# Selective scan: a different order of work ahead of the first scan, and other slots for the layer norm of later rows

## The chip, the cores and the metric

The kernel runs on one core of a Trainium2 chip. The metric is the device time of one execution in microseconds (us), as the median of several runs. A core has five engines with queues of their own, each of which works strictly in the order of its queue: PE (TensorE, matrix products), DVE (VectorE), ACT (ScalarE, activation functions), POOL (GpSimd) and SP (SyncE, which here only issues transfers). They wait for one another through semaphores.

## The reference

The program is a chain of four layers on a tensor of 2 images x 128 channels x 64 x 64 pixels: an attention layer, a convolution layer with deformed sampling, three residual steps of 3x3 convolutions, and a selective scan. The change lies in the last one. Cut to what matters, for an image x of L = 4096 pixels and C = 128 channels, run in four pixel orders:

```
xn = (x - mean(x)) * rsqrt(mean((x - mean(x))**2) + 1e-5) * w + b   # over the 128 channels
xh, z = split(xn @ W_in.T)                   # 256 channels each
xh = silu(causal_conv4(xh))                  # along the order
dt, B, C = split(xh @ W_xp.T)                # 8, 16 and 16 columns
dt = softplus(dt @ W_dt.T + b_dt)            # 256 channels
h[t] = exp(dt[t] * A) * h[t-1] + dt[t] * B[t] * xh[t]     # 256 channels x 16 states
y[t] = sum over states (h[t] * C[t]) + xh[t] * Dp
out  = (y * silu(z)) @ W_out.T
```

The four results are fused by one more product and added to x.

## The kernel before, in words

`layer3` (from line 1121) holds the scan. An image is cut into NBLK = 8 *blocks* of 512 pixels (8 image rows); with 2 images and 4 orders there are 64 blocks, worked off in one row: blocks 0 to 31 are image 0, 32 to 63 are image 1. Of an image, two orders go along the rows and two along the columns. The normalized image lies in two tiles: `xn`, by rows, and `xt`, by columns. Image 0 is normalized into `xn` and turned into `xt` by copies (`turn`, L1260); image 1 the other way round.

**Layer norm of one block of rows** is a chain of eight parts over four engines: `ln_mean` (PE, L1216, a product with a matrix of 1/128), `ln_less` (DVE, L1226, x minus mean), `ln_square` (ACT, L1229), `ln_var` (PE, L1233), `ln_log` (ACT, L1237), `ln_root` (ACT, L1240), `ln_scale` (POOL, L1243, the product of x minus mean and the root), `ln_store` (ACT, L1252). `ln_mean` and `ln_var` write to the PSUM tile called `da`, which rotates through three buffers and is also the one that the scan's decay factors use.

**The front of a block** makes what its scans need: `conv` (PE, L1294), `conv_silu` (ACT, L1299, with a table load before and one after), `xproj` (PE, L1318), `xproj_copy` (ACT, L1324 and L1326), `bc_store` (transfer of B and C to DRAM, L1330), `delta` (PE, L1345), `softplus` (ACT, four activations, L1351 to L1354), `sum_parts` (PE, L1359), `sum_copy` (ACT, L1362), `spread` (POOL, L1367, dt times xh), `xproj_rest` and `rest_copy` (PE L1336 and L1337, ACT L1340), `zproj` and `zproj_silu` (L1306, L1312). `spread_store` writes dt and dt times xh of one half of 128 channels to DRAM (L1372, 512 KB), and `spread_load` reads them back in eight transfers (L1381, 256 KB each), so that each partition holds one channel and one state of a group of four. `copies` reads B or C back, each row onto 32 partitions, in four transfers a group (L1401).

**The scan.** Each block has 8 *groups* (2 halves of channels x 4 groups of states), each of four scans. A group takes: `weights` (PE, L1391, B onto the partitions through PSUM), `db_dve` and `db_pool` (DVE L1412 and POOL L1421 share the product of B and dt times xh: the table `ND` says how many of four quarters are DVE's, for the eight groups 4, 0, 1, 4, 4, 4, 0, 4), `expo` (ACT, L1429, four decay factors), `scan` (DVE, L1438, four), `keep` (ACT, L1443, the last states, to `hl`), `cmul` (POOL, L1448, the states times C, over all four quarters), `sums` (PE, L1456). `gate`, `project` and `finish` end a block.

**The order is written out by hand**: inside `tc.manual_schedule()` each engine gets its instructions in program order. The main loop runs over all 512 groups and a few steps more; step k is group k % 8 ("slot") of block i = k // 8. In its slots the front of block i+1 is worked on (`front_pe`, `front_act`, `front_pool`, `transfers`), and from slot 5 on the convolution of block i+2. `expo` runs two scans ahead (AHEAD = 2); in its rotation of three `da` buffers a layer norm takes one whenever `ln_mean` or `ln_var` is due. `next_norm` says which rows' layer norm, if any, goes beside block i: in the kernel before these are the eight of image 1, beside blocks 22 to 29.

Ahead of the loop stands the *prologue*: a loop over t = 0 to 9 takes all eight layer norms of image 0, one behind the other, with the front of block 0 laid between them (slot = t - 2), and then the convolution of block 1. Five of the six sets of `copies` of block 0, `db_pool(1)` and the first two `expo` follow. The second half's `spread_load` of block 0 is issued in slot 0 of the main loop.

Of the kernel before, what the change touches and what calls it, by code (L numbers as in the profile page):

```python
# [25 lines left out]
NBLK = L // BLK  # L26
# [1094 lines left out]
def layer3(g, I, out):  # L1121
# [12 lines left out]
    with ExitStack() as ctx:  # L1134
# [70 lines left out]
        xn = a.tile([P, HW + 2 * HB, HW], F32, name="xn")  # L1205
        xt = a.tile([P, L + 2 * HC], F32, name="xt")
        N = {}


        def ln_tile():  # L1210
# [5 lines left out]
            nc.tensor.matmul(N[k, "mean"], onesm, interior(g, b, k * RB, RB), start=True, stop=True)  # L1216

        def ln_less(b, k):
            if b == 0:

                t = wk.tile([P, 4, BLK], F32, name="db")
                N[k, "xc"], N[k, "sq"] = t[:, 0, :], t[:, 1, :]
            else:
                N[k, "xc"] = ck.tile([P, BLK], F32, name="xc", bufs=1)
                N[k, "sq"] = ck.tile([P, BLK], F32, name="sq", bufs=1)
            nc.vector.tensor_sub(img(N[k, "xc"]), interior(g, b, k * RB, RB), img(N[k, "mean"]))  # L1226

# [100 lines left out]
        def bc_store(i):  # L1328
            S[i]["bx"] = dr.tile([2 * N_STATE, BLK], F32, name="bx")
            nc.sync.dma_start(S[i]["bx"], S[i]["xd"][: 2 * N_STATE])  # L1330
# [38 lines left out]
        def spread_store(i, hf):  # L1369

            S[i]["dx", hf] = dr.tile([P, 2, BLK], F32, name="dx")
            nc.sync.dma_start(S[i]["dx", hf], S[i].pop(("dd", hf)))  # L1372
# [11 lines left out]
        def weights(k):  # L1384

            i, hf, ng = groups[k]
            G[k] = {}
            if ND[hf][ng] == 0:
                return
            pb = psb.tile([P, BLK], F32, name="pbc")  # L1390
            nc.tensor.matmul(pb, sel[:, ng].rearrange("p j c -> p (j c)"), S[i]["bc"], start=True, stop=True)  # L1391
            G[k]["pb"] = pb
# [15 lines left out]
        def db_dve(k):  # L1408
            i, hf, ng = groups[k]
            n = ND[hf][ng]  # L1410
            if n:
                nc.vector.tensor_tensor(  # L1412
                    db_tile(k)[:, :n, :], G[k].pop("pb").unsqueeze(1).to_broadcast([P, n, BLK]),
                    S[i]["d4", hf][:, 1, :n, :], ALU.mult,
                )

        def db_pool(k):
            i, hf, ng = groups[k]
            n = ND[hf][ng]
# [113 lines left out]
        def front_pe(i, slot):  # L1533
            if i < NBK:
                if slot == 0:
                    xproj(i)
                elif slot == 1:
                    delta(i, 0)
                    delta(i, 1)
                elif slot == 2:  # L1540
                    sum_parts(i, 0)
                elif slot == 3:
                    sum_parts(i, 1)
                    xproj_rest(i)
                elif slot == 4:
                    zproj(i)
            if i + 1 < NBK:
                if slot == 5:
                    begin(i + 1)
                elif slot == 6:  # L1550
                    conv(i + 1, 1)

        def front_pool(i, slot):
            if i < NBK:
                if slot in (3, 4):
                    spread(i, slot - 3)

        def next_norm(i):

            b, k = divmod(i, 4 * NBLK)  # L1560
            k -= 4 * NBLK - 2 - NBLK
            return (b + 1, k) if b + 1 < NB and 0 <= k < NBLK else None

        with tc.manual_schedule():
            tc.keep_in_program_order(nc.scalar.preload_act_table_set("natural_log_exp_and_others"))
            nc.scalar.activation(am, am, AF.Exp)
            nc.vector.tensor_scalar(am, am, -1.0, None, ALU.mult)
            nc.vector.memset(xt[:, :HC], 0.0)
            nc.vector.memset(xt[:, HC + L :], 0.0)
            nc.vector.memset(xn[:, HB - 1, HW - HC :], 0.0)  # L1570
            nc.vector.memset(xn[:, HB + HW, :HC], 0.0)

            for t in range(NBLK + 2):
                slot = t - 2
                if slot == 6:
                    for k in range(2):
                        weights(k)
                    db_dve(0)
                    db_pool(0)
                if slot >= 0:  # L1580
                    front_pe(0, slot)
                    front_act(0, slot)
                    front_pool(0, slot)
                if slot == 1:
                    bc_store(0)
                elif slot in (3, 4):
                    spread_store(0, slot - 3)
                    if slot == 3:
                        spread_load(0, 0)
                        copies(0, "b", 0)  # L1590
                        copies(0, "c", 0)
                if t < NBLK:
                    for part in (ln_mean, ln_less, ln_square):
                        part(0, t)
                if 0 <= t - 1 < NBLK:
                    for part in (ln_var, ln_log, ln_root, ln_scale, ln_store):
                        part(0, t - 1)
                if t == 1:
                    begin(0)
                    conv(0, 1)  # L1600
                    conv_silu(0)
            for ng in range(1, NNG):
                copies(0, "b", ng)
                copies(0, "c", ng)
            db_pool(1)
            units = [(k, q) for k in range(len(groups)) for q in range(4)]
            AHEAD = 2
            for u in range(AHEAD):
                expo(*units[u])
            for k in range(len(groups) + 7):  # L1610
                i, slot = divmod(k, 8)
                live = k < len(groups)
                more = k + 1 < len(groups)
                ended = 1 <= k <= len(groups)
                transfers(i + 1, slot)
                if k + 2 < len(groups):
                    weights(k + 2)
                norm = next_norm(i)
                for q in range(4):
                    if slot == 6 and q == 3 and 1 <= i <= NBK:  # L1620
                        finish(i - 1)
                    if norm and slot == 3 and q == 3:
                        ln_log(*norm)
                    if 4 * k + q + AHEAD < len(units):
                        expo(*units[4 * k + q + AHEAD])
                    if norm and q == 0:
                        if slot == 0:
                            ln_mean(*norm)
                        elif slot == 3:
                            ln_var(*norm)  # L1630
                    if q == 0 and ended:
                        keep(k - 1)
                    if live:
                        scan(k, q)

                    for j, hf in (((k - 6) // 8, 0), ((k - 10) // 8, 1)):
                        if q == 1 and 8 * j + 6 + 4 * hf == k and 0 <= j < NBK:
                            gate(j, hf)
                if norm and slot == 0:
                    ln_less(*norm)  # L1640
                if more:
                    db_dve(k + 1)
                if ended:
                    cmul(k - 1)
                if k + 2 < len(groups):
                    db_pool(k + 2)

                if slot == 5 and 0 <= k - 2 < len(groups):
                    sums(k - 2)
                if slot == 5 and 1 <= i <= NBK:  # L1650
                    project(i - 1)
                front_pe(i + 1, slot)
                front_act(i + 1, slot)
                front_pool(i + 1, slot)
                if norm:
                    if slot == 1:
                        ln_square(*norm)
                    elif slot == 3:
                        ln_root(*norm)
                    elif slot == 4:  # L1660
                        ln_scale(*norm)
                    elif slot == 6:
                        ln_store(*norm)
                if live:

                    if slot == 6 and i % (4 * NBLK) < NBLK // 2:
                        for n in range(2):
                            turn(blocks[i][0], 2 * (i % (4 * NBLK)) + n)

                if slot != 5 and 0 <= k - 2 < len(groups):  # L1670
                    sums(k - 2)
# [160 lines left out]
```

## Time and profile before

| | |
|---|---|
| median of 3 runs | 5844.72 us (5840.14 to 5851.18) |
| the profiled execution, its own time | 5845.92 us |
| its span, first to last instruction | 5844.1 us |
| end of the layer before (last activation into `xa`) | 2453.66 us |
| first scan (L1438) | 2523.73 us |
| block 0's last gate (L1465) | 2585.33 us |
| a usual block, gate to gate | 51.56 us |
| nine blocks from 3612.62 to 4097.33, among them those with a layer norm | 484.71 us |

Times inside the execution are counted from the start of its span. The gate of a block's second half is read at slot 2 of the next block, so "block by block" below means from one such gate to the next. In the lists of waits, "A <- B: x, n, y" says that A waited for B for x us in n waits, the longest y us. In a timeline each line has start, duration, engine, line, operation and names, with the idle time of the engine before it and what ended it in brackets.

### The profile page before, as it was taken

To read this page: it belongs to the slowest core of one execution; us is meant where nothing else is said; L and a number is where in the kernel's file an instruction comes from. 1 tells how busy PE (TensorE), PEld (TensorE's weight loads), DVE (VectorE), ACT (ScalarE), POOL (GpSimd) and SP (SyncE) were. 2 spreads that over 40 slices of the span, in tenths; PEclk is the share of its full clock that TensorE was granted. 3 is DMA by queue.
4 is the path that set the end of the run, shared out by engine and by line. 5 is a ranking of instruction groups with operands and counts; after the bars stand their busy time and mean duration, and the time that the engine had idled before them with its cause. 6 is when DMAs were issued, how large, how long until landed. Compare 5 with 4: busy or idle time off the path is not lost.

```text
span 5844.1 us, 57551 instructions
## 1 busy us (share of the span) xinstructions
PE 4898.7 (84%) x19110; PEld 1732.8 (30%) x19110; DVE 4430.6 (76%) x4138; ACT 3829.3 (66%) x5499; POOL 3621.2 (62%) x1136
## 2 busy tenths in 40 slices
PE   7999999989978779877777878777787777778776
PEld 3333333334434334322222222222222222222221
DVE  5333333355124589679999999999999999999998
ACT  4888888840025521277777777777777777777775
POOL 5111111100010021079999999999999999999998
PEclk8999999999989889988888888888888888888886
DMA  5000001030056300055555565555555565555564
GB/s 156 19 19 19 19 19 33 1 59 1 1 101 112 76 12 0 6 136 130 136 130 131 142 141 130 121 133 143 137 135 128 131 141 141 133 131 132 134 141 101
DMA packets 333105, 541.88 MB, mean 93 GB/s; under 512 B 66384, under 2 KB 121184, under 8 KB 331712
## 3 DMA queue, kind: packets, MB, share of 16 engines
q1 hardware_dynamic: 329664, 534.58, 39.3%
q10 hardware_dynamic: 3136, 3.56, 0.2%
q8 instruction: 151, 2.47, 0.2%
q14 instruction: 154, 1.26, 0.1%
HBM read 448.81 MB, written 89.13 MB: 92 GB/s over the span
## 4 chain that ended last, share of the span: by engine, by line
DVE 50%; PE 37%; issue 5%; POOL 3%; DMA 2%; ACT 2%; SPq 1%; DVEq 0%; POOLq 0%; ACTq 0%
DVE db L1438 36%; DVE db L1412 12%; PE ps L287 11%; PE acc L303 9%; PE m L1052 6%; PE m L566 5%; PE acd L812 2%; DVE gt L1465 1%; PE m L526 1%; POOL db L1448 1%; PE pf L775 1%; POOL db L1421 1%; PE pc L663 1%; DMA hats<-pos 1%; SPq L748 1%
## 5 line engine op out<-in xcount | busy, mean ns | idle before, releaser
L1448 POOL TENSOR_TENSOR db<-db,c 128x2048 f32<-128x2048 f32 x512 | 2309.6, 4530 | 57.1 <-ACT hl L1443 52.0
L1438 DVE TENSOR_TENSOR_SCAN db<-da,hl,db 128x512 f32<-128x512 f32 x1792 | 2155.0, 1263 | 47.6 <-ACT da L1429 9.5
L1429 ACT ACTIVATE da<-dd,am 128x512 f32<-128x512 f32 x2048 | 1402.1, 688 | 824.3 <-DVE db L1438 814.5
L293 ACT ACTIVATE e<-ps 128x1024 f16<-128x1024 f32 x1024 | 992.3, 1021 | 135.7 <-PE ps L287 123.9
L1456 PE MATMUL py<-db,fold 128*32 128x512 f32 x4096 | 618.1, 689 | 234.8 <-POOL db L1448 231.9
L1421 POOL TENSOR_TENSOR db<-b,dd 128x2048 f32<-128x2048 f32 (+1 forms) x192 | 799.1, 4162 | 0.0
L1412 DVE TENSOR_TENSOR db<-pbc,dd 128x2048 f32<-128x2048 f32 (+1 forms) x384 | 767.3, 1998 | 0.6 <-PE pbc L1391 0.6
L314 DVE RECIPROCAL rec<-acc 32x512 f32<-32x512 f32 x64 | 214.9, 3358 | 640.3 <-PE acc L303 640.3
L321 POOL TENSOR_TENSOR parts<-parts 32x512 f32<-32x512 f32 x64 | 80.4, 1256 | 976.3 <-DVE parts L320 976.3
L287 PE MATMUL ps<-q,k 32*128 32x512 f32 x4096 | 656.4, 643 | 3.5 <-DVE flag L250 2.7
L303 PE MATMUL acc<-e,v 128*128 128x512 f16 x2048 | 532.2, 383 | 0.0
L1052 PE MATMUL m<-v,u 128*128 128x512 f32 x864 | 378.6, 601 | 50.6 <-DVE v L1021 50.6
L1359 PE MATMUL pm<-dd,ident 128*128 128x512 f32 x512 | 362.0, 845 | 4.6 <-ACT dd L1352 4.4
L1391 PE MATMUL pbc<-bc,sel 64*128 64x512 f32 x384 | 209.8, 546 | 162.8 <-DVE db L1412 162.6
L1318 PE MATMUL pm<-u,wxp 128*72 128x512 f32 x256 | 197.6, 917 | 175.0 <-ACT u L1299 175.0
L303 PEld LDWEIGHTS <-v 128*128 128x128 bf16 x2048 | 158.6, 97 | 510.6 <-issue 389.4
L1438 DVE TENSOR_TENSOR_SCAN db<-da,db 128x512 f32<-128x512 f32 x256 | 292.5, 1204 | 18.7 <-ACT da L1429 12.1
L287 PEld LDWEIGHTS ps<-q,k 32*128 32x128 f32 x4096 | 229.6, 183 | 228.3 <-issue 170.0
L1456 PEld LDWEIGHTS py<-db,fold 128*32 128x32 f32 x4096 | 90.4, 114 | 623.8 <-POOL db L1448 364.9
L566 PE MATMUL m<-comb,w 64*128 64x512 f32 (+4 forms) x1296 | 269.9, 575 | 0.0
L1294 PE MATMUL pm<-xn,wcs 128*128 128x512 f32 x512 | 236.9, 606 | 22.3 <-ACT xa L1483 7.5
L686 POOL TENSOR_SCALAR yt<-y 32x512 f32<-32x512 f32 x8 | 18.2, 2271 | 381.7 <-DVE y L677 381.3
(317 smaller groups left out, 6026.7 us busy)
## 6 DMA issues: line engine op xcount, KB each, us to landing
dd<-dx SPq DMA_DIRECT2D x1024, 256.0 KB, 6.4
dx<-dd SPq DMA_DIRECT2D x128, 512.0 KB, 3.4
c<-bx SPq DMA_DIRECT2D x1024, 64.0 KB, 2.1
hats<-pos SPq DMA_DIRECT2D x136, 256.0 KB, 9.7
b<-bx SPq DMA_DIRECT2D x512, 64.0 KB, 4.5
q<-qd SPq DMA_DIRECT2D x32, 512.0 KB, 7.4
w<-in_conv0T SPq DMA_DIRECT2D x18, 288.0 KB, 8.5
q<-in_x SPq DMA_DIRECT2D x8, 512.0 KB, 7.1
```

Of the source, the lines that this page charges most:

```text
L287: nc.tensor.matmul(ps[:, i, :], k4[h % 2][rows, kb // 4, :], q4[h % 2][rows, qb * BLK : (qb + 1) * BLK], start=True, stop=True,)
L293: nc.scalar.activation(e[:, :n, :], ps[:, :n, :], AF.Exp)
L303: nc.tensor.matmul(acc, v3[b][:, kb, h, :], e[:, i, :], start=(kb == 0), stop=(kb == NS - 1))
L566: yield lambda q=q, dy=dy, src=src, i0=i0, i1=i1: nc.tensor.matmul(m[:, i0 * NF : i1 * NF], w[half, dy, q, x, :], src, start=(dy == KC and ...
L1052: nc.tensor.matmul(m[x], weights[j][:, dy, x, :], v[j][b][:, x, r0 : r0 + RP, :].rearrange("p r i -> p (r i)"), start=(dy == 0), stop=(dy ...
L1359: nc.tensor.matmul(ps, g.ident, S[i]["dd", hf][:, x, :], start=(x == 0), stop=(x == 1))
L1412: nc.vector.tensor_tensor(db_tile(k)[:, :n, :], G[k].pop("pb").unsqueeze(1).to_broadcast([P, n, BLK]), S[i]["d4", hf][:, 1, :n, :], ALU.mult,)
L1421: nc.gpsimd.tensor_tensor(db_tile(k)[:, n:, :], S[i]["b", ng].unsqueeze(1).to_broadcast([P, 4 - n, BLK]), S[i]["d4", hf][:, 1, n:, :], ALU ...
L1429: nc.scalar.activation(da, S[i]["d4", hf][:, 0, q, :], AF.Exp, scale=am[:, hf, q, ng : ng + 1])
L1438: nc.vector.tensor_tensor_scan(d1, d0, d1, 0.0 if first else hl[:, hf, ng, q, :], ALU.mult, ALU.add)
L1448: nc.gpsimd.tensor_mul(v, v, S[i]["c", ng].unsqueeze(1).to_broadcast([P, 4, BLK]))
L1456: nc.tensor.matmul(S[i]["y", hf][32 * q : 32 * q + 32, :], fold, G[k]["db"][:, q, :], start=False, stop=(ng == NNG - 1),)
```

## The change

There are four parts.

1. **The prologue is written out anew.** Only the first NFIRST = 3 layer norms of image 0 are taken there, in an order of their own. The front of block 0 follows, then all `copies` of block 0, then the last pieces of the front, with the silu of block 1's convolution behind the first two `expo`. On SP's queue the second half's `spread_store` now stands ahead of all `copies`.
2. **The other five layer norms of image 0** (rows 3 to 7) go beside blocks 0 to 4: `next_norm(i)` gives `(0, 3 + i)` for i < 5. They use the small tiles `xc` and `sq` (one buffer each) that image 1's use, not a `db` tile.
3. **Inside a block with a layer norm**, `ln_var` moves from the start of slot 3 to that of slot 2, `ln_log` from the last quarter of slot 3 to that of slot 2, and `ln_scale` from slot 4 to slot 5. `ln_root` (slot 3), `ln_square` (slot 1), `ln_mean` and `ln_less` (slot 0) and `ln_store` (slot 6) stay. This holds for both images.
4. **The turning copies** (two of `turn` in slot 6 of four blocks) go beside blocks 1 to 4 of an image, not 0 to 3.

The arithmetic is the same.

```
         def ln_less(b, k):
-            if b == 0:
+            if b == 0 and k < NFIRST:
...
         def next_norm(i):
+            if i < NBLK - NFIRST:
+                return 0, NFIRST + i
             b, k = divmod(i, 4 * NBLK)
...
-            for t in range(NBLK + 2):
-                slot = t - 2
...
-                if t < NBLK:
-                    for part in (ln_mean, ln_less, ln_square):
-                        part(0, t)
-                if 0 <= t - 1 < NBLK:
-                    for part in (ln_var, ln_log, ln_root, ln_scale, ln_store):
-                        part(0, t - 1)
...
+            for k in range(NFIRST):
+                ln_mean(0, k)
+            for k in range(NFIRST):
+                ln_less(0, k)
+            ln_square(0, 0)
+            ln_var(0, 0)
+            ln_square(0, 1)
+            ln_log(0, 0)
+            ln_root(0, 0)
+            ln_scale(0, 0)
+            ln_var(0, 1)
+            ln_square(0, 2)
+            ln_store(0, 0)
+            ln_var(0, 2)
+            begin(0)
+            conv(0, 1)
+            for part in (ln_log, ln_root, ln_scale):
+                for k in (1, 2):
+                    part(0, k)
+            conv_silu(0)
+            front_pe(0, 0)
+            ln_store(0, 1)
+            front_act(0, 0)
+            bc_store(0)
+            front_pe(0, 1)
+            front_act(0, 1)
+            ln_store(0, 2)
+            sum_parts(0, 0)
+            sum_copy(0, 0)
+            spread(0, 0)
+            spread_store(0, 0)
+            spread_load(0, 0)
+            softplus(0, 1)
+            front_pe(0, 3)
+            front_act(0, 3)
+            spread(0, 1)
+            spread_store(0, 1)
+            for ng in range(NNG):
                 copies(0, "b", ng)
                 copies(0, "c", ng)
+            for k in range(2):
+                weights(k)
+            db_dve(0)
+            db_pool(0)
+            front_pe(0, 4)
+            front_act(0, 4)
+            front_pe(0, 5)
+            front_pe(0, 6)
             for u in range(AHEAD):
                 expo(*units[u])
+            front_act(0, 7)
+            db_pool(1)
...
-                    if norm and slot == 3 and q == 3:
+                    if norm and slot == 2 and q == 3:
                         ln_log(*norm)
...
-                        elif slot == 3:
+                        elif slot == 2:
                             ln_var(*norm)
...
-                    elif slot == 4:
+                    elif slot == 5:
                         ln_scale(*norm)
...
-                    if slot == 6 and i % (4 * NBLK) < NBLK // 2:
+                    if slot == 6 and 0 < i % (4 * NBLK) <= NBLK // 2:
                         for n in range(2):
-                            turn(blocks[i][0], 2 * (i % (4 * NBLK)) + n)
+                            turn(blocks[i][0], 2 * (i % (4 * NBLK) - 1) + n)
```

More of the change, by code (lines that the diff above doesn't have):

```diff
@@ L1207, in layer3 @@
         N = {}
+        NFIRST = 3
         def ln_tile():
@@ L1571, in layer3 @@
             nc.vector.memset(xn[:, HB + HW, :HC], 0.0)
-            for t in range(NBLK + 2):
-                slot = t - 2
[L1575 to L1591, printed above, removed]
-                if t < NBLK:
-                    for part in (ln_mean, ln_less, ln_square):
-                        part(0, t)
-                if 0 <= t - 1 < NBLK:
-                    for part in (ln_var, ln_log, ln_root, ln_scale, ln_store):
-                        part(0, t - 1)
[L1598 to L1601, printed above, removed]
@@ L1602, in layer3 @@
-            for ng in range(1, NNG):
+            units = [(k, q) for k in range(len(groups)) for q in range(4)]
+            AHEAD = 2
+            for k in range(NFIRST):
[11 more added lines that the diff above has]
+            ln_store(0, 0)
@@ L1603, in layer3 @@
+            spread_load(0, 0)
[5 more added lines that the diff above has]
+            for ng in range(NNG):
                 copies(0, "b", ng)
                 copies(0, "c", ng)
-            db_pool(1)
-            units = [(k, q) for k in range(len(groups)) for q in range(4)]
-            AHEAD = 2
+            for k in range(2):
+                weights(k)
+            db_dve(0)
+            db_pool(0)
```

## Prediction

> **What bounds the kernel now.** I read the page first (busy time and the 40 slices), then busy time by stage, then timelines of the prologue and of blocks with a layer norm. From the page:
>
> ```profile
> PE 4898.7 (84%) x19110; PEld 1732.8 (30%) x19110; DVE 4430.6 (76%) x4138; ACT 3829.3 (66%) x5499; POOL 3621.2 (62%) x1136
> ...
> DVE  5333333355124589679999999999999999999998
> POOL 5111111100010021079999999999999999999998
> ```
>
> From slice 17 on, the scan layer, DVE and POOL are both full; before it DVE isn't. By stage (span, then busy us of PE, PEld, DVE, ACT, POOL):
>
> ```profile
> core 0: us, PE busy (x) PEld busy (x) DVE busy (x) ACT busy (x) POOL busy (x), PEclk, DMA share, GB/s
> ...
> 2453.66:2523.73 70.07, 54.01 (x106) 19.80 (x107) 15.79 (x36) 42.18 (x61) 18.02 (x12) 0.87 0.35 91
> ...
> 3561.06:3612.62 51.56, 42.59 (x122) 13.11 (x121) 50.94 (x41) 38.19 (x63) 50.83 (x14) 0.80 0.58 134
> 3612.62:4097.33 484.71, 377.99 (x1123) 115.39 (x1122) 463.85 (x370) 362.18 (x591) 465.97 (x126) 0.85 0.55 131
> ```
>
> The first row is the prologue: 70.07 us in which no engine is full; a chain sets it. The second is a usual block: 50.94 of 51.56 us on DVE, which sets the time, and 50.83 on POOL, which has 0.7 us left. The third is nine blocks with image 1's eight layer norms. Without norms they would take 462.1 (seven of 51.56 and two, where an order begins, of 50.95 and 50.23, as the same places show in other orders); they take 22.6 more, 2.8 a norm, and only 0.6 of that is `ln_less` on DVE.
>
> The prologue, SP's and ACT's queues in the timeline:
>
> ```profile
> 2495.84 0.33 SPq L1372 DMA_DIRECT2D dx<-dd  x1
> 2498.66 3.65 SPq L1381 DMA_DIRECT2D dd<-dx  x8
> ...
> 2507.15 0.34 SPq L1372 DMA_DIRECT2D dx<-dd  x1
> ...
> 2518.32 0.81 ACT L1252 ACTIVATE xn<-db,vecs 128x512 f32<-128x512 f32 x1 [1.37 <-POOL db L1243]
> 2519.14 1.28 ACT L1299 ACT_TABLE_LOAD   x1
> ...
> 2523.01 2.67 ACT L1429 ACTIVATE da<-dd,am 128x512 f32<-128x512 f32 x4
> ```
>
> SP stores block 0's first half at 2495.84 and loads it back; the loads of this stretch landed one by one, the last at 2510.8 (8.8 after its issue). DVE began `db_dve(0)` at 2511.2, so all but the decay factor was there at 2513.5. But ACT still had layer norms 5 to 7 and block 1's silu in its queue, and began `expo` only at 2523.01. Norms cost at both ends: they hold the front of block 0 back (`xd` copied at 2476.71, but the last product stored 19 us later), and then `expo`.
>
> A block with a layer norm, around slots 3 and 4:
>
> ```profile
> 3781.72 2.08 PE L1233 MATMUL da<-sq,onesm 128*128 128x512 f32 x2 [0.54 <-DVE db L1438]
> 3787.19 0.59 ACT L1362 COPY dd<-pm 128x512 f32<-128x512 f32 x1 [1.37 <-PE pm L1359]
> 3789.36 0.57 ACT L1340 CAST bc<-pm 32x512 fp32r<-32x512 f32 x1 [1.59 <-PE pm L1337]
> 3791.20 2.34 DVE L1438 TENSOR_TENSOR_SCAN db<-da,db 128x512 f32<-128x512 f32 x2 [1.57 <-ACT da L1429]
> 3791.37 4.54 POOL L1448 TENSOR_TENSOR db<-db,c 128x2048 f32<-128x2048 f32 x1 [2.59 <-ACT hl L1443]
> ```
>
> and the waits over all nine such blocks (total us, times, longest):
>
> ```profile
> POOL db L1448 <- ACT hl L1443: 18.2, 8, 4.5
> DVE db L1438 <- ACT da L1429: 11.3, 14, 1.6
> ACT bc L1340 <- PE pm L1337: 10.4, 8, 1.8
> ```
>
> The reader is to see the chain: `ln_var` stands ahead of `sum_parts` on PE in slot 3, so `rest_copy` waits on ACT for PE (eight times); behind it in ACT's queue are `ln_root`, `expo` and `keep`, so DVE misses its decay factor (1.57) and POOL the states (2.59). POOL has no room for that: 8 x 4.53 (`cmul`) + 12.5 (`db_pool`) + 2 x 1.26 (`spread`) + 1.26 (`ln_scale`) = 52.5 us.
>
> **What the Trainium skill says.** "GPSIMD Engine Reference", section 3.1: a tensor_tensor of 2048 fp32 takes 4497 ns on GpSimd and 2293 ns on VectorE; this trace has 4530 and 2292. "ScalarE: Activation LUTs", What ACT_TABLE_LOAD costs: about 1283 ns and a drain of 1380; the trace has 1283, and the next activation starts at once (2520.43 after 2519.14), so I count 1.28. "DMA: Bandwidth & Descriptors", Two DMAs through the same engine are not ordered: a transfer that reads what another wrote must wait on its semaphore. The trace agrees: SP waits 2.3 us for the store before it loads. "TensorE: Matmul & The Clock Gate", What's actually happening: the array is slow until some 3.4 us of activity. Here the first four passes take 0.94 us each, those of the convolution 0.43.
>
> **The change, part by part.**
>
> *Prologue up to the first product.* Nothing before 2457.5 moves. A third `ln_mean` (two passes) joins the first two; it ends near 2459, when the weights for L1164 land. `ln_var(0)` now stands ahead of the transposes: instead of 2462.8 I have 2461 to 2462, `xn`'s first rows at 2465.4 to 2466 (was 2467.5). The convolution needs `wcs` too, whose second half came at 2467.8; it ends at 2472.5 to 2473.8 (was 2474.7). Then ACT: u until 2473.3, table 1.28, `ln_store` 0.8, `xd` 0.58 at 2475.4, `bc` to 2476.5: at most 1 us sooner than now. From here, no norms lie between. `delta` after `bc`: 0.45 + 0.6, then four activations (2.5, from 2482.12 to 2484.63), to 2480.1; `sum_parts`' second product 1.2, `sum_copy` 0.57, `spread` 1.27: 2483.2, against 2495.84. Range 2482.5 to 2486.
>
> *To the first scan.* From that point the present run has store 2.7, first load at 2.8, last landing at 15.0, `db_dve(0)` 15.4 to 17.7. These stay, since what is now behind the loads (a 512 KB store in place of 64 KB copies) is issued after them. First scan: 2483.2 + 17.8 = 2501.0. ACT isn't late: four loads have landed at 10.8 (2494), two `expo` take 1.3, block 1's silu with two tables 3.9, so the third `expo` ends before 2500. Against 2523.73: **-22.7**.
>
> *Start-up of block 0.* SP seems to issue a transfer once the one eight before it landed (the store at 2507.15 follows the fifth load's landing at 2507.09). So `copies` of B for group 1, now behind a store that lands near 17.1 after the product, land at 19.5; `db_pool(1)` takes 4.5, to 24.0, while DVE, 4.6 of scans and 0.66 of `ln_less` after 17.8, wants it at 23.0: a stall of 1. From there POOL is behind: by adding its queue up, with `ln_scale`, `db_pool` of block 1's slot 2 ends 62 after the first scan, not 59.4, and the gate comes at 63.8, not 61.6: **+2.2**. The second half's loads, behind 24 copies, would be issued from 26 and land by 38; `db_dve(4)` wants them at 40. This margin is thin.
>
> *Norms beside blocks 1 to 4.* A norm is two products on PE (two passes each), one DVE, four ACT (0.6 + 0.7 + 0.6 + 0.8 = 2.7) and one POOL instruction, with no transfers; five of them leave the prologue. `xc` and `sq` have one buffer, but `ln_less` follows the `ln_store` before it by more than a slot. DVE: 51.56 + 0.6 and the 0.26 to 0.8 that it waits in slot 1, where `ln_mean` delays `xproj` (seen now too): 52.5 to 52.9. POOL: 52.5. I take 52.8: 4 x 1.25 = **+5.0**. On ACT, Ln and Square add 1.1 in slots 1 and 2, and the buffer that `ln_var` takes puts one `expo` after a scan more: the `expo` for slot 3's third scan, now ready 1.5 ahead, is ready 0.3 ahead. `keep` of slot 2 is as near to its `cmul`. Both I cost at nothing; without that cover, see rival 1. In slot 6 `ln_store` waits some 2 us on ACT for the later `ln_scale`; behind it are two turning copies (2.0), then `expo` for slot 7's third scan: 0.8 us of cover.
>
> *Image 1's norms.* With `ln_var` in slot 2, `sum_parts` and `xproj_rest` in slot 3 are done about 2 us sooner, `keep` at 3789 instead of 3791.2, so POOL's waits (18.2) and most of DVE's on ACT (11.3) go. POOL alone would be 8 x 52.5; blocks 25 and 29, which show only 0.25 us of POOL's idle time, took 53.04 and 52.28. With 52.8 and 52.0 for the block before: 474.4 against 484.7: **-10.3**. `turn` for image 1 costs nothing now and nothing then.
>
> *Sum*: -22.7 + 2.2 + 5.0 - 10.3 = -25.8. On the profiled execution that is 5845.92 - 25.8 = 5820.1 (span 5818.3); its time is 1.2 above the median, so the forecast is **5818.9**.
>
> **Rivals.** *1. A new wait in slot 2.* The cover of 0.3 us isn't there, and ACT holds DVE or POOL up by 1 us in each of 13 norms: -25.8 + 13 = -12.8, 5832. For it: softplus, Ln, Square stand in one row. Against: at present ACT waits for DVE in slot 2 (up to 1.0 us). 14%. *2. The transfers set the start.* Copies in front of the second half's loads make block 0 wait, or the store slows the first loads: the prologue gives 15 instead of 22.7, or block 0 costs 10: 5826. For it: 2 us of margin only. Against: in the present run those loads needed 11.5. 15%. *3. The move of `ln_var` does nothing*, since POOL is the bound at any rate: image 1's blocks gain 2 only, 5827. Against: POOL idled in six of eight. 8%. *4. Slower.* Each norm beside a block costs much more than now. Eight norms cost 22.6; thirteen at x would cost 13x. The prologue gives 22.7 less 1 of start-up, so it is a loss from x = 44.3 / 13 = 3.4. Mechanism: the later `ln_scale`, behind one `cmul` of 4.5 more, keeps ACT in `ln_store`, and with it `expo` and `keep` in slot 7. I put the delay at 2.2 and the cover at 3; at a delay of 5.5 or more x passes 3.4. At 4 a norm: 5852. For it: POOL's lag is my sum. 3%.
>
> **How the numbers follow.** The likeliest case, 60%, has 5811 to 5826 (product 0 to 3 later, norms 1.0 to 1.5 each). Rivals 1 to 3 lie at 5826 to 5832. Low end 5806: norms at POOL's own 52.5, all eight stalls gone. High end 5831. A measurement can tell about 0.2%, 11.7 us, so the border is at 5833.0: half of rival 1 lies beyond it; faster 0.90, same 0.07, slower 0.03.
>
> **What would show it.** First scan at 2499 to 2504; block 0's gate about 20 us earlier; blocks 1 to 4 at 52.3 to 53.2; nine blocks near 474, with POOL's waits for `hl` under 5 us; no wait of ACT for L1337's product. I'd be wrong with DVE waits for ACT in slot 3, or for L1381's landing in block 0, or with POOL idle behind `keep` of slot 6.

## The result, and the profile after

The changed kernel takes **5813.48 us** in the median of five runs (5811.19 to 5818.12), against 5845.71 (5840.14 to 5851.18) for the kernel before, run beside it: 32.2 us less, a ratio of 0.9945 with a 95% interval of 0.9933 to 0.9957. The forecast was 5818.9. The profiled execution took 5815.21, its span is 5813.4 (before: 5845.92 and 5844.1).

From the pages, the costliest row in which something changed, before and after, and a row of DVE (busy us, mean ns of one, then idle time ahead and what ended it):

```profile
L1448 POOL TENSOR_TENSOR db<-db,c 128x2048 f32<-128x2048 f32 x512 | 2309.6, 4530 | 57.1 <-ACT hl L1443 52.0
```

```profile
L1449 POOL TENSOR_TENSOR db<-db,c 128x2048 f32<-128x2048 f32 x512 | 2310.8, 4532 | 36.5 <-ACT hl L1444 33.8
...
L1413 DVE TENSOR_TENSOR db<-pbc,dd 128x2048 f32<-128x2048 f32 (+1 forms) x384 | 766.5, 1996 | 32.0 <-DMA dd<-dx 32.0
```

POOL's waits for the kept states make up 33.8 us of a whole execution, against 52.0 before. The 32.0 us in the last row is one wait, DVE's for the first loads of block 0. The first scan now follows those loads and the product behind them; in the kernel before it waited for ACT for another 10.28 us after that product. By stage (span, then busy us of PE, PEld, DVE, ACT, POOL, then PE's granted clock, the DMA share and GB/s), from the end of the layer before:

```profile
2452.44:2500.78 48.34, 40.40 (x83) 14.90 (x83) 12.01 (x32) 29.46 (x41) 6.28 (x5) 0.89 0.37 94
2500.78:2565.30 64.52, 45.85 (x133) 14.68 (x134) 62.45 (x53) 49.46 (x84) 61.20 (x17) 0.82 0.67 157
2565.30:2774.83 209.53, 167.93 (x500) 52.93 (x499) 205.79 (x164) 167.40 (x272) 208.09 (x57) 0.83 0.56 132
...
3595.72:4066.98 471.26, 373.56 (x1123) 118.06 (x1122) 461.89 (x370) 362.51 (x591) 466.02 (x126) 0.85 0.57 135
...
4066.98:5804.23 1737.25, 1352.22 (x4045) 413.54 (x4044) 1708.94 (x1350) 1266.38 (x2071) 1715.13 (x438) 0.83 0.56 133
```

These are the prologue, block 0, blocks 1 to 4, the nine blocks with image 1's norms, and all that follows. Set beside before:

| stage (us) | before | after | difference | forecast |
|---|---|---|---|---|
| end of the layer before | 2453.66 | 2452.44 | -1.2 | 0 |
| from there to the first scan | 70.07 | 48.34 | -21.7 | -22.7 |
| first scan to block 0's gate | 61.60 | 64.52 | +2.9 | +2.2 |
| blocks 1 to 4 | 206.22 | 209.53 | +3.3 | +5.0 |
| blocks 5 to 20 | 821.07 | 820.89 | -0.2 | 0 |
| nine blocks, 21 to 29 | 484.71 | 471.26 | -13.5 | -10.3 |
| blocks 30 to 63 | 1738.42 | 1737.25 | -1.2 | 0 |

The four stages that the change touches give -29.0. The rest of the difference between the two spans (-30.7), about 2 us, lies in stages that it doesn't touch: the end of the layer before falls anywhere from 2447.96 to 2455.62 in the profiles below, in kernels that are the same up to there. So the experiments are read by stage first.

The prologue of the changed kernel in the timeline, SP, ACT and DVE together:

```profile
2482.94 0.33 SPq L1373 DMA_DIRECT2D dx<-dd  x1
2485.78 3.81 SPq L1382 DMA_DIRECT2D dd<-dx  x8
...
2493.91 1.30 ACT L1430 ACTIVATE da<-dd,am 128x512 f32<-128x512 f32 x2
2495.22 1.28 ACT L1300 ACT_TABLE_LOAD   x1
...
2498.38 2.29 DVE L1413 TENSOR_TENSOR db<-pbc,dd 128x2048 f32<-128x2048 f32 x1 [31.97 <-DMA dd<-dx]
2500.78 4.57 DVE L1439 TENSOR_TENSOR_SCAN db<-da,db 128x512 f32<-128x512 f32 x4
```

The product is stored 30.5 after the layer before (before: 42.2), and the first scan comes 17.8 later (before: 27.9). The first two `expo` are done at 2495.21; DVE waits for the loads alone.

And the waits of the nine blocks (total us, times, longest); the first three were 10.4, 18.2 and 11.3 before:

```profile
ACT bc L1341 <- PE pm L1338: 5.3, 6, 1.5
...
POOL db L1449 <- ACT hl L1444: 5.0, 7, 2.4
...
DVE db L1439 <- ACT da L1430: 3.5, 5, 1.1
...
DVE db L1439 <- POOL db L1422: 0.3, 1, 0.3
```

POOL's 5.0 is no more than blocks without a norm have: in blocks 13 to 21 of the same profile the same wait adds up to 4.7. A norm's price can be read off here. Nine blocks without norms take 462.1; the excess is 9.2, or 1.15 a norm (before: 22.6, 2.8 a norm). It adds up on DVE: eight `ln_less` of 0.66 are 5.3, the waits for ACT 3.5 and for `db_pool` 0.3, together 9.1. This is a rough account, since blocks without norms have waits of DVE too (0.6 for ACT in blocks 13 to 21).

### The profile page after: what moved, and what is told of

Same layout as the page of the kernel before. It is cut to its first block, busy times and chain, and to the rows that moved or that the text cites. A ratio compares the mean times of both kernels' runs of the same rounds, so it can differ in the third digit from the quotient of the medians.

```text
span 5813.4 us, 57554 instructions
## 1 busy us (share of the span) xinstructions
PE 4881.1 (84%) x19110; PEld 1732.0 (30%) x19110; DVE 4427.0 (76%) x4138; ACT 3827.3 (66%) x5499; POOL 3620.8 (62%) x1136
## 3 DMA queue, kind: packets, MB, share of 16 engines
q14 instruction: 154, 1.26, 0.1%
## 4 chain that ended last, share of the span: by engine, by line
DVE 50%; PE 37%; issue 4%; POOL 3%; DMA 3%; ACT 2%; SPq 1%; DVEq 0%; POOLq 0%; ACTq 0%
DVE db L1439 35%; DVE db L1413 11%; PE ps L287 11%; PE acc L303 9%; PE m L1052 6%; PE m L566 5%; PE acd L812 2%; DVE gt L1466 1%; PE m L526 1%; POOL db L1449 1%; POOL db L1422 1%; PE pf L775 1%; PE pc L663 1%; DMA c<-bx 1%; SPq L748 1%
## 5 line engine op out<-in xcount | busy, mean ns | idle before, releaser
L1449 POOL TENSOR_TENSOR db<-db,c 128x2048 f32<-128x2048 f32 x512 | 2310.8, 4532 | 36.5 <-ACT hl L1444 33.8
L1295 PE MATMUL pm<-xt,wcs 128*128 128x512 f32 x512 | 235.6, 602 | 24.6 <-ACT xa L1484 15.4
L686 POOL TENSOR_SCALAR yt<-y 32x512 f32<-32x512 f32 x8 | 18.2, 2271 | 381.7 <-DVE y L677 381.4
```

Source lines behind the costliest of these rows:

```text
L1449: nc.gpsimd.tensor_mul(v, v, S[i]["c", ng].unsqueeze(1).to_broadcast([P, 4, BLK]))
```

## The experiments

In the diffs that follow, "+" is the experiment. The lines are those of the changed kernel, in two cases (said there) of the kernel before.

**Part 3 alone, both ways round.** `e1_old_slots` takes the slots back in the changed kernel:

```
-                    if norm and slot == 2 and q == 3:
+                    if norm and slot == 3 and q == 3:
                         ln_log(*norm)
...
-                        elif slot == 2:
+                        elif slot == 3:
                             ln_var(*norm)
...
-                    elif slot == 5:
+                    elif slot == 4:
                         ln_scale(*norm)
```

> The changed kernel with its third part undone: ln_var and ln_log in slot 3, ln_scale in slot 4, the new prologue and the norms beside blocks 0 to 4 kept. Theory (the order in slots 2 and 3 is what costs): the nine blocks with image 1's norms go from 471.3 back to 482 to 486 us, POOL waits some 18 us for the kept states there again, blocks 1 to 4 of image 0 go from 209.5 to 214 to 218, and the first scan stays 48.3 after the end of the layer before; about 5813.5 + 13 + 6 = 5832. Rival (the nine blocks gained because they come at another place in time, or POOL is the bound at any rate): they stay at 470 to 473, and the whole at 5814 to 5818.

Measured: median 5835.69 over ten runs (5824.89, the profiled one, to 5839.13), ratio to before 0.9981 (0.9972 to 0.9991). Nine blocks take 480.71, 9.5 more than in the changed kernel, blocks 1 to 4 take 214.72, and the first scan comes 48.19 after the layer before. Its nine blocks, by stage and then by waits:

```profile
3596.36:4077.07 480.71, 371.34 (x1123) 113.64 (x1122) 463.18 (x370) 362.27 (x591) 465.87 (x126) 0.87 0.56 132
```

```profile
POOL db L1449 <- ACT hl L1444: 12.9, 8, 2.7
...
DVE db L1439 <- ACT da L1430: 7.7, 10, 1.1
```

The old slots bring the old waits back (12.9 and 7.7, against 5.0 and 3.5), in image 0's blocks as well, where they cost 5.2 over four norms. That rules out that POOL is the bound whatever the slots are. The profiled execution is the fastest of the ten and has the highest granted clock over the whole execution, 0.891. The median of the ten lies 22.2 above the changed kernel's, of which the stages of this profile explain 14.6, so the 9.5 is likely at the low end; no other execution was traced. The forecast for its nine blocks was 482 at least; the kernel before has the same slots there and took 484.71. The column after the busy times, the granted clock of PE, may be why: with the old slots the nine blocks took 484.71 at 0.85, 482.76 at 0.86 (e12, below) and 480.71 at 0.87, while with the new slots they took 471.26 at 0.85 and 471.23 at 0.84. The products that ACT waits for in slot 3 are PE's. But this is three profiles with the old slots, and no run set the clock by itself.

`e3_slots_alone` is the reverse of this diff, on the kernel before.

> The kernel before with only the third part of the change: ln_var and ln_log in slot 2, ln_scale in slot 5; its own prologue with all eight norms. Theory: the nine blocks at 470 to 473 us instead of 484.7, all else as before (first scan 70 after the end of the layer before): 5845.7 - 13.5 = 5832, a ratio of 0.9977. Rival (the gain needs the other parts too): nine blocks above 478.

Measured: median 5831.23 over twelve runs against 5845.57, ratio 0.9977 (0.9969 to 0.9986), so -14.3. Nine blocks take 471.23; first scan, block 0 and blocks 1 to 4 stand as before (69.80, 61.59, 206.18). Part 3 is worth 13.5 there, by stage, without any other part, and needs none of them. In the changed kernel it is worth 9.5 to 13.5 in the nine blocks, depending on which profile with the old slots is taken, and 5.2 in blocks 1 to 4. Without it block 0 and blocks 1 to 4 lose 3.0 and 8.5 against the kernel before, for a prologue that gives 21.9.

`e2_scale4` takes back only the third of the three moves.

```
-                    elif slot == 5:
+                    elif slot == 4:
                         ln_scale(*norm)
```

> The changed kernel with ln_scale alone moved back to slot 4, ln_var and ln_log left in slot 2. Theory (ln_var carries the gain, ln_scale's place is free either way): nine blocks at 470 to 473 us, ACT no longer waits for POOL ahead of ln_store (2.6 us now), blocks 1 to 4 at 208 to 211. Rival (ln_scale a slot later is part of the gain, since POOL reaches its product of slot 3 sooner): nine blocks at 475 or more.

Measured: 5819.41 in one run; nine blocks 471.57, blocks 1 to 4 209.85, block 0 65.51 (64.52 in the changed kernel). So `ln_var` and `ln_log` carry part 3, and the place of `ln_scale` makes no difference in a running block. In block 0 it may be worth up to 1.0: there POOL waits 1.15 for the fourth `cmul`'s states instead of 0.47. It is one profile each, and block 0 took 65.14 in a kernel that does less in it (`e10_no_scale`, below).

**What the five norms cost.** `e4_no_norms` leaves the norms of rows 3 to 7 of image 0 out and fills those rows with zeros:

```
         def next_norm(i):
-            if i < NBLK - NFIRST:
-                return 0, NFIRST + i
...
+            nc.vector.memset(xn[:, HB + NFIRST * RB : HB + HW, :], 0.0)
```

> The changed kernel without the five norms beside blocks 0 to 4: the layer norm of rows 3 to 7 of image 0 is left out, with zeros in its place, written by one memset on DVE while it waits for transfers. It prices the five norms. Theory: blocks 1 to 4 at 206.2 us (209.5 with the norms), block 0 from first scan to gate at 62 to 63.5 (64.5 now), the nine blocks of image 1 as now; some 5 us less in all. Rival (the norms are free beside the scans, and what blocks 0 to 4 have over 51.56 is something else): 209 and 64.5 stay.

Measured: 5815.02 in one run. Blocks 1 to 4 take 206.53 and block 0 62.59; the memset, 2.19 us on DVE between the two copies of `wcs`, held the convolution back, so its first scan, 49.80 after the layer before, isn't to be compared. Five norms cost 3.0 in blocks 1 to 4 and 1.9 in block 0: 1.0 each. (Block 0's stage ends in slot 2 of block 1, so it holds two of the five `ln_less`, 1.3 of the 1.9.) Its block 0 is still 1.0 longer than before's, with no norm in it, and the timeline shows where:

```profile
2509.46 4.57 DVE L1439 TENSOR_TENSOR_SCAN db<-da,db 128x512 f32<-128x512 f32 x4 [0.90 <-POOL db L1422]
...
2522.60 4.54 POOL L1449 TENSOR_TENSOR db<-db,c 128x2048 f32<-128x2048 f32 x1 [0.82 <-ACT hl L1444]
```

That is the start-up alone, and `e12_old_order`, below, which has no norm there either, shows the same stall (0.80): `db_pool` begins 0.93 after the first scan (2504.93 after 2504.00), and DVE finds it 0.90 late at the fifth. In the changed kernel it begins 0.60 after, and `ln_less` stands in just this place and fills the gap.

**Where block 0 loses its time.** The changed kernel's block 0, POOL, ACT and DVE together:

```profile
2501.38 7.90 POOL L1422 TENSOR_TENSOR db<-b,dd 128x2048 f32<-128x2048 f32 x2 [13.28 <-DMA b<-bx]
...
2514.94 0.69 ACT L1430 ACTIVATE da<-dd,am 128x512 f32<-128x512 f32 x1 [0.58 <-DVE db L1439]
2515.57 0.67 ACT L1238 ACTIVATE sq<-da,cst 128x512 f32<-128x512 f32 x1
...
2520.53 4.54 POOL L1449 TENSOR_TENSOR db<-db,c 128x2048 f32<-128x2048 f32 x1 [2.15 <-ACT hl L1444]
...
2564.10 1.28 DVE L1439 TENSOR_TENSOR_SCAN db<-da,hl,db 128x512 f32<-128x512 f32 x1 [1.12 <-POOL db L1422]
```

`db_pool` starts 0.6 after the first scan, when B lands, and DVE is not held up by it: its fifth scan runs at 2505.92 without a wait. But in slot 2 ACT first waits 0.58 for a scan, with `expo` for the third scan, as `ln_var` has taken one of the three `da` buffers; then comes Ln (0.67), and from there to `keep` of slot 2 ACT has no gap. POOL waits 2.15 for the states. In the kernel without these norms `expo` has no such wait and no Ln follows it, and POOL waits 0.82. (Square, in slot 1, is not the cause: the wait of 0.58 comes behind it.) From then on POOL has one more gap, of 0.47, and at block 1's slot 2 `db_pool` comes 1.12 late for DVE. The account of block 0 closes: DVE's busy time is 62.45 against 60.87 (two more `ln_less`), and its waits are 1.3 where before had none.

`e6_copies_first` tests whether an earlier B helps. It issues B of groups 1 and 2 and C of group 0 ahead of the product:

```
             bc_store(0)
+            copies(0, "b", 1)
+            copies(0, "c", 0)
+            copies(0, "b", 2)
...
-            for ng in range(NNG):
-                copies(0, "b", ng)
+            for ng in (1, 2, 3):
                 copies(0, "c", ng)
```

> The changed kernel with block 0's copies for db_pool(1), db_pool(2) and the first cmul issued right behind bc_store, in the time in which SP waits for the first product, instead of behind both stores. It asks what block 0's start-up cost is made of. Theory: db_pool(1) waits no longer for B (13.3 us of POOL idle, ended by that landing, at 2501.4) but for the last load, 3 us sooner; POOL isn't behind at the end of block 0, and block 0 from first scan to gate takes 62.3 to 63 instead of 64.5; the first scan stays at 48.3. Rival (the norm in block 0 fills POOL whatever its start): 64 or more. Loss, if any: the twelve issues hold up the first store, by up to 1 us.

Measured: 5815.81 in one run, first scan 47.77, block 0 63.91. POOL:

```profile
2499.83 7.93 POOL L1422 TENSOR_TENSOR db<-b,dd 128x2048 f32<-128x2048 f32 x2 [9.44 <-DMA dd<-dx]
2509.24 4.51 POOL L1449 TENSOR_TENSOR db<-db,c 128x2048 f32<-128x2048 f32 x1 [1.48 <-ACT hl L1444]
2515.17 4.53 POOL L1449 TENSOR_TENSOR db<-db,c 128x2048 f32<-128x2048 f32 x1 [1.42 <-ACT hl L1444]
2521.86 4.54 POOL L1449 TENSOR_TENSOR db<-db,c 128x2048 f32<-128x2048 f32 x1 [2.16 <-ACT hl L1444]
```

POOL starts 2.4 ahead of the first scan instead of 0.6 behind it, and loses nearly all of it again in front of `cmul`, to `keep` (1.48, 1.42, 2.16). Block 0 gains 0.6 of the 2.4, which is no more than this stage differs between kernels with the same prologue (65.14 in e10, below); the expectation was 62.3 to 63. When B arrives is not what decides.

**Is the first scan bound by the loads?** `e5_product_first` loads dt times xh ahead of dt, so that `db_dve` may start on the first four of eight loads:

```
         def spread_load(i, hf):
...
-            for x in range(2):
+            for x in (1, 0):
```

> The changed kernel with one edit: the loads of dt times xh go ahead of those of dt (the loop over x in spread_load runs 1, 0). It asks what sets the first scan now. Theory (the landing of the last of eight loads, then db_dve's 2.3 us and no more): db_dve(0) starts when the fourth load lands, some 4 us sooner after the first load, and the first scan follows the eighth landing by 0.7 (expo) instead of 2.4 (db_dve): first scan 46.5 to 47.2 after the end of the layer before instead of 48.3. Rival (ACT's queue sets it as before the change): no difference, or later, since expo now waits for the last load and block 1's silu behind it with two table loads comes later: 48.3 or more, or a stall at the third scan.

Measured: 5814.71 in one run, first scan 46.30 after the layer before (-2.0), block 0 66.99 (+2.5). DVE:

```profile
2492.13 2.29 DVE L1413 TENSOR_TENSOR db<-pbc,dd 128x2048 f32<-128x2048 f32 x1 [26.65 <-DMA dd<-dx]
2497.77 2.34 DVE L1439 TENSOR_TENSOR_SCAN db<-da,db 128x512 f32<-128x512 f32 x2 [3.34 <-ACT da L1430]
2502.96 2.34 DVE L1439 TENSOR_TENSOR_SCAN db<-da,db 128x512 f32<-128x512 f32 x2 [2.86 <-ACT da L1430]
```

`db_dve` starts 5.3 us sooner, counted from the layer before, but now the decay factor's loads come last: DVE waits 3.34 for the first `expo`, and 2.86 before its third scan, since `conv_silu` of block 1 with both its table loads stands on ACT behind the first two `expo`. In the changed kernel this silu lies under the wait for the loads and the product. Both theories had a true half: the loads do bound the first scan, and what is won there is given back, since ACT's queue behind it was fitted to that wait.

**How the prologue's gain divides.** `e12_old_order` is the kernel before, its order kept, with only three norms in the prologue; the norms of rows 3 to 7 of image 0 are left out, and their rows are zeros:

```
+            nc.gpsimd.memset(xn[:, HB + 3 * RB : HB + HW, :], 0.0)
...
-                if t < NBLK:
+                if t < 3:
...
-                if 0 <= t - 1 < NBLK:
+                if 0 <= t - 1 < 3:
```

> The kernel before, its own order of the prologue, with the layer norms of rows 3 to 7 of image 0 left out (zeros in their place, by a memset on POOL ahead of its first product). It splits the prologue's gain of 21.7 us into what leaves it and the new order. By the timeline of the kernel before: the first half's spread ends at 2492.8 instead of 2495.8, since norm 2 still stands between the two softplus and norm 3 no longer does; the first scan follows 17.7 behind, 56.9 after the end of the layer before: 13 us by what leaves, 8.6 by the order. Rivals: the order gives nothing (48 to 50), or the five norms give nothing without it (66 or more).

Measured: 5828.49 in one run; first scan 56.13 after the layer before, block 0 62.50, nine blocks 482.76. DVE's line of its start:

```profile
2506.44 2.29 DVE L1412 TENSOR_TENSOR db<-pbc,dd 128x2048 f32<-128x2048 f32 x1 [29.47 <-DMA dd<-dx]
```

Of the 21.7, then, 13.9 come from the five norms leaving, and 7.8 from the order written out. The product is stored 42.2 after the layer before in the kernel before, 38.5 here, 30.5 in the changed kernel: the order's whole gain is ahead of that store. The norms' leaving gave 3.7 ahead of it and 10.2 behind it, where `expo` had waited in ACT's queue. The parts are those of this order of steps: the new order with all eight norms was not run.

**What still limits a block with a norm.** Three kernels ask whether it is POOL, ACT or `ln_mean`. `e10_no_scale` leaves `ln_scale` of all norms beside blocks out (`ln_store` takes x minus mean unscaled):

```
-                    elif slot == 5:
-                        ln_scale(*norm)
```

> The changed kernel without ln_scale for the norms that stand beside blocks (the product of x minus mean and the root is left out; rows 3 to 7 of image 0 and all of image 1 are stored unscaled). It asks whether POOL's 1.26 us is what a norm costs now. If POOL is the bound beside norms: the nine blocks fall from 471.3 to 467 to 468, which is ln_less alone over 462.1. If DVE's own 0.6 and its waits for ACT in slot 1 carry the cost: they stay at 469.5 to 471.5.

Measured: 5814.36 in one run; nine blocks 470.65 (-0.6), block 0 65.14. Waits of the nine:

```profile
POOL db L1449 <- ACT hl L1444: 12.5, 10, 2.2
...
DVE db L1439 <- ACT da L1430: 3.3, 5, 1.1
```

POOL has 8.8 us less to do (457.20 against 466.02) and waits 7.5 more: it isn't what sets these blocks. DVE's waits stay.

`e11_log_twice` puts one more `ln_log` into slot 2 of every block with a norm:

```
                     if norm and slot == 2 and q == 3:
                         ln_log(*norm)
+                        ln_log(*norm)
```

> The changed kernel with ln_log issued twice in slot 2 (the same result, 0.57 to 0.67 us more on ACT for each norm). It asks how much cover slot 2 has. By the prediction's count (0.3 us of cover for the expo of slot 3's third scan and for keep): DVE or POOL waits 0.3 us a norm more, the nine blocks at 473 to 475 instead of 471.3. If slot 2 has more room than counted: 471 to 472. If it has none: 476 or more.

Measured: 5825.21 in one run; nine blocks 475.17, so 3.9 more, or 0.5 for each 0.7 that was added to ACT (368.17 busy against 362.51); blocks 1 to 4 take 2.1 more.

```profile
POOL db L1449 <- ACT hl L1444: 9.1, 9, 2.4
...
DVE db L1439 <- ACT da L1430: 4.8, 12, 0.8
```

DVE's waits for ACT are now twelve, not five, and 4.8 us in place of 3.5. As much again is paid by way of POOL: it waits 4.1 longer for the states, and DVE's waits for `db_pool` go from 0.3 to 1.7. By the difference, 0.7 added and 0.5 paid, I estimate some 0.2 us of room left on ACT in slot 2.

`e8_mean_late` moves `ln_mean` behind `xproj` on PE, out of the way of block i+1's front, and `ln_less` to slot 1:

```
-                        if slot == 0:
-                            ln_mean(*norm)
-                        elif slot == 2:
+                        if slot == 2:
...
+                    if norm and slot == 1 and q == 1:
+                        ln_less(*norm)
...
-                if norm and slot == 0:
-                    ln_less(*norm)
...
                     front_pe(i + 1, slot)
+                if norm and slot == 0:
+                    ln_mean(*norm)
```

> The changed kernel with ln_mean behind xproj on PE at the end of slot 0 and ln_less after the second scan of slot 1. It asks what a norm still costs: 1.15 us each in the nine blocks, of which ln_less is 0.6. Theory (ln_mean, which waits for a scan on PE ahead of xproj, makes ACT and then DVE late in slot 1; DVE's waits for ACT are 3.5 us there): they go, nine blocks at 467.5 to 469.5 instead of 471.3, blocks 1 to 4 at 208 to 209. Rival (POOL's 52.5 is the bound): nine blocks at 470.5 or more, DVE's waits turn into waits for db_pool.

Measured: 5818.89 in one run; nine blocks 473.70 (+2.4). DVE's waits for ACT fall from 3.5 to 2.3, those for `db_pool` rise from 0.3 to 3.5: what is taken from one comes back in the other. The theory (467.5 to 469.5) failed. What the new place costs shows on ACT: it now waits 5.0 us, in five blocks, for the product of `delta`, which stands behind `ln_mean` on PE; the changed kernel has no such wait.

`e9_all` has the edits of e5, e6 and e8 together.

> The edits of the three runs before it together. If they add up: first scan 47 after the end of the layer before, block 0 at 62.5, blocks 1 to 4 at 208.5, nine blocks at 468.5, some 7 us below the changed kernel, 5806, a ratio to the kernel before of 0.9933. If POOL's load is the bound beside the norms: 5810.

Measured: median 5816.10 over five runs (5812.46 to 5821.96) against 5846.52, ratio 0.9949 (0.9935 to 0.9963): first scan 46.23, block 0 67.02, nine blocks 474.94. The three edits don't add up (5806), and the time is above the rival's 5810 as well. No better than the changed kernel, and nothing tried here is.

## Why the prediction was right, and where it wasn't

The direction, the size and the order of the four terms were right; the sum was -25.8 where -29.0 was measured in the same stages. The terms were off by +1.0, +0.7, -1.7 and -3.2, so errors of both signs met in it.

- **Prologue.** Right but for one step. `db_dve` started 15.4 after the product's store and the first scan 17.8 after it, both as forecast. That the store came at 2482.94, forecast 2483.2, is in part luck: the layer before ended 1.2 sooner in this profile, and from that end the store took 30.5 where 29.5 was forecast. The 1.0 is in `sum_parts`. Its second product was to end 1.2 after the softplus, as in the kernel before; it ended 2.2 after. The four passes took 3.41 us where they had taken 2.40. In every profile with three norms in the prologue they take 3.35 to 3.8, in both with eight 2.40; why, no run tests. The claim that loads decide is shown by e5, where `db_dve` followed its loads forward.
- **Start-up of block 0.** The size was near (+2.9 against +2.2), and so was the place where DVE pays (`db_pool` of block 1's slot 2, 1.12 late). But what puts POOL behind is another step, so the size is in part luck. The prediction said that the copies of B land late, that DVE stalls 1 for `db_pool(1)`, and that POOL's queue carries this on. B landed 0.6 after the first scan, not 1.7, and the fifth scan didn't stall. A stall of 0.8 to 0.9 appears only where no norm fills the place (e4, e12), so 1.0 of the 2.9 is start-up and 1.9 the norms. What put POOL behind was the cover costed at nothing, "`keep` of slot 2 is as near to its `cmul`": Ln, and the `expo` that waits for a buffer, ahead of it cost POOL 1.3 there. The second half's loads, the thin margin, came in time: no wait of DVE for them.
- **Norms beside blocks 1 to 4.** The mechanism stood, the term was too large: 52.8 a block was forecast and 52.4 measured. Of the missing 1.7 over the four blocks, 0.7 is a matter of counting, since one of the four `ln_less` falls into block 0's stage. For the rest, the prediction counted DVE's waits for ACT in every such block, where they occur five times in nine blocks. And it took POOL's 52.5 as a floor. These four blocks have 208.09 busy on POOL, 52.0 each: durations in a row overlap a little in the trace (two `db_pool` of 4.52 and 3.44 take 7.90), and the prediction's own line of a usual block, 50.83, with `ln_scale` added gives 52.1. By e10, in the nine blocks, POOL isn't what sets the time.
- **Image 1's norms.** The same term again: 52.8 was taken, 52.4 came out, so -13.5 in place of -10.3. This is the largest miss of the four. The chain itself (`ln_var` ahead of `sum_parts` in slot 3, then `rest_copy`, then `expo` and `keep`) agrees with e1 and e3: the slots alone give and take the time, and the waits go and come with them. By e2 it is `ln_var` and `ln_log` that do it; which of the two was not tested. "No wait of ACT for L1337's product" was wrong: 5.3 of 10.4 remain, in six blocks, while DVE waits for ACT only 3.5 in all.
- **The cover in slot 2.** "Ready 0.3 ahead" was about right for the running blocks: from e11 I estimate the room at some 0.2.

Three readings of the kernel before were slightly off, and changed nothing. The fourth of its eight loads landed 9.9 after the store, not 10.8; when DVE began `db_dve(0)`, norms 6 and 7 were left on ACT, not 5 to 7; and 2292 ns is the first of DVE's products alone, the mean of that size being 2265.

The rivals: the new wait in slot 2 (1) did not come in the running blocks, though e11 shows how near it is. The transfers (2) do set the first scan, but on time, and neither block 0's loads nor the store delayed anything. That moving `ln_var` does nothing because POOL is full (3) falls by e1, e3 and e10. The slower case (4) needed 3.4 a norm, and a norm costs 1.0 to 1.15. Its mechanism is there, `ln_store` of block 0 holds ACT up by 1.52 at 2542.76, but what lies behind has cover.

What stays open is the difference of about 3 us between the medians (-32.2) and the touched stages (-29.0). The layers ahead of the scan, which are the same in all these kernels, differ by up to 7.7 us from profile to profile, so one profile each can't settle it. The place of the turning copies (part 4) was not tried by itself. And why the nine blocks with the old slots took 480.71 in one kernel and 484.71 in another isn't settled, beyond the clock that goes with it.

## What to carry over

Beside a full engine a step's place in the queues can matter more than its length: the same norm cost 2.8 us with its second product standing ahead of `sum_parts`, and 1.15 with that product and `ln_log` one slot earlier. Before a wait at the start of a stage is shortened, look at what was laid under it: the silu under the wait for the loads came out as a new wait as soon as the loads allowed an earlier start. And an engine that is busy 99% of a stage need not bound it: take its work away in one run and see whether the time follows.

## What the runs showed of the hardware

- A transfer behind others in SP's queue can be issued late although SP has nothing else to do: behind the eight loads and the second half's store, four copies of 64 KB took from 2490.73 to 2494.87 to issue, and the next four waited until 2495.79; four such copies further on took 1.81. The trace shows what holds them: the transfers of this program report on eight semaphores in turn, and SP waits, before it issues one, for the landing of the transfer eight places ahead, which used the same semaphore (6.1 us in seven waits there). This comes from the program's own waits.
- The eight loads of 256 KB land one after the other, 1.1 to 1.3 us apart (2492.04 to 2498.16 for the third to the eighth).
- A memset of 128x2560 fp32 takes POOL 2.23 us (e12) and DVE 2.19 us (e4), while a tensor_tensor of 128x2048 fp32 takes them 4.53 and 2.26. POOL is as fast as DVE in the memset and half as fast in the tensor_tensor.
- The same scan of 128x512 takes 1.20 us when its start is the constant 0 and 1.26 when it is read from `hl`.
